# Four score matmuls of one burst: the two even key tiles first, then the two odd ones

## The chip, the cores and the metric

The kernel runs on one core of one Trainium2 chip. The metric is device time in microseconds (us) of one launch. Three runs of the kernel before gave 11260.99, 11263.95 and 11266.25 us, and the median, 11263.95 us, is the time before. Engines are named as in the profile: PE is TensorE's matmul and PEld its weight load, DVE is VectorE, ACT is ScalarE, POOL is GpSimd, SP is SyncE.

## The reference

Four graph layers follow one another on x (3327 rows, 128 columns) with one dense matrix adj (3327 by 3327). The change lies in layer 0, which takes almost all of the time. Cut to what matters (h is the normed x, and spatial_encoding and edge_encoding are both adj):

```python
q = (h @ Wq.T).reshape(d, n, heads_h)      # d = 128, n = 3327, heads_h = 8
k = (h @ Wk.T).reshape(d, n, heads_h)
v = (h @ Wv.T).reshape(d, n, heads_h)
a = jnp.einsum('dnh,dmh->dnm', q, k) * d ** -0.5
a = a + adj + adj
a = jax.nn.softmax(a, axis=2)
out = jnp.einsum('dnm,dmh->dnh', a, v).reshape(n, heads_h * d)
x = x + out @ Wo.T
```

So there are 128 heads, each with a contraction over only 8 elements, and for every head a 3327 by 3327 matrix of scores, of which every element goes through an exponential. Layers 1 to 3 are three more products with adj or its transpose and some elementwise work.

## The kernel before

**Tiles.** Scores are made transposed: keys lie on the 128 partitions, queries along the free dimension. There are 26 key tiles of 128 keys, taken as 13 pairs of an even and an odd tile (`NQ = 13`), 7 chunks of 476 queries (`NC`, `CW`; the last has 472), and 32 groups of 4 heads (`NG`). One unit of work, `u`, is (chunk, group, pair of key tiles): 7 x 32 x 13 = 2912 units. Each unit goes through its 4 heads j = 0 to 3 one after the other.

**One unit's banks.** A unit holds two of seven PSUM banks of the tile S, one for its even and one for its odd key tile (`banks(u)`). DVE first copies the adjacency of the tile into the bank (`seed`, L660). Then, for each head, PE adds the scores on top of what is in the bank (`scores`, L666), and ACT reads the bank and writes the exponential to SBUF (`exps`, L678 for both banks in one instruction of 128 x 952, L681 where the two banks don't lie side by side in the right order or one is left to DVE, 128 x 476). Heads 1 to 3 don't begin from the seed again: the queries' tile QS holds the negated query of the head before beside the new one, so the matmul takes the old head's score out of the bank and adds the new one. So a head's score matmul has to wait for the exponential of the head before on the same bank, and head 0's for the seed.

**Row halves.** A score matmul contracts over 64 rows only (two f32r halves of query and key, and old and new head). The even key tile's operands lie in partitions 0 to 63, the odd one's in partitions 64 to 127 (`KT[b][64 * r:64 * r + 64, ...]`, r = 0 even, r = 1 odd). The two therefore use the upper and the lower half of the array's rows.

**Values.** With the exponentials as moving operand, PE sums out the values and the softmax's denominator (`values`, L719): for one key tile four matmuls of 9 columns, one for each head, each at another 32-column group of the array, into one bank `po`. DVE empties `po` after the 13 units of a group (`store`, L727). In three of 13 units the odd tile's exponential of head 0 is worked out on DVE as a polynomial (`hand_exp`, L692 to L703).

**The order of the work.** It is written out by hand under a manual schedule: each engine runs its instructions in the order in which the loop issues them. The loop runs over slots i. ACT has one (unit, head) per slot: unit u has its heads in slots 4u, 4u + 3, 4u + 6 and 4u + 9 (`in_slot`). PE's work is issued in odd slots: a burst of four score matmuls, for the slots i + 1 and i + 2, then the values of one key tile of an earlier unit:

```python
if at % 2:
    for k in (1, 2):
        u, j = in_slot(i + k)
        if 0 <= u < n:
            scores(u, j)
    u, r = ((i - 11) // 4, 0) if at == 3 else ((i - 13) // 4, 1)
    if 0 <= u < n:
        values(u, r)
```

One call of `values` is one key tile of one unit, four matmuls; each f32 matmul of them leaves two records. So one burst and its values make one PE cycle: four records of L666, then eight of L719. There are two such cycles for each unit, 5824 in all.

Names for what follows: in a burst, A is the unit and head of slot i + 1 and B those of slot i + 2. Ae is A's even tile, Ao its odd one, Be and Bo are B's. Before, the burst runs Ae, Ao, Be, Bo. A and B are different units and never share a bank. In the bursts with i % 4 = 3, A is a unit's head 0, so that Ae and Ao wait for the two seeds; in all others A waits for the exponential of slot i - 2. B always waits for the exponential of slot i - 1. `touch` sets these dependencies bank by bank.

Of the kernel before, what the change touches and what calls it, by code (L numbers as in the profile page):

```python
# [22 lines left out]
P = 128  # L23
# [15 lines left out]
NG = HEADS // 4  # L39
# [41 lines left out]
def width_of(c):  # L81

    return min(CW, N + 1 - c * CW)
# [8 lines left out]
def gnn_kernel(ctx: ExitStack, tc: tile.TileContext, x, adj, Wq, Wk, Wv, Wo, embed, layer,  # L92
               embed_bias, layer_bias, weight, bias, W_in, W_out, out):
    nc = tc.nc
# [174 lines left out]
    class Square:  # L269
# [29 lines left out]
        def store(self, to=by_tile):  # L299
            nc.sync.dma_start(to[:, :, self.s * P:(self.s + 1) * P].rearrange("t p n -> p t n"), self.cols)  # L300
# [152 lines left out]
    with tc.tile_pool(name="d1", bufs=1) as d1, tc.tile_pool(name="d2", bufs=2) as d2, \  # L453
# [17 lines left out]
        with tc.If(loose > 0):  # L471
            for s in range(squares_of(0), NT):
                square(d2, s, d2)
            for t in range(NT):
# [5 lines left out]
                with tc.For_i(0, HEADS, 1) as d:  # L480
# [3 lines left out]
                    for r in range(2):  # L484
                        for b in range(4):
# [4 lines left out]
                                             start=True, stop=True)  # L490
# [9 lines left out]
            for c in range(NC):  # L500
                c0 = c * CW
                w = min(CW, N - c0)
# [3 lines left out]
                with tc.For_i(0, HEADS, 1) as d:  # L506
# [12 lines left out]
                    for t in range(NT):  # L519
# [8 lines left out]
                                         start=(t == 0), stop=(t == NT - 1))  # L528
# [9 lines left out]
    with tc.tile_pool(name="e1", bufs=1) as e1, tc.tile_pool(name="e_adj", bufs=30) as e_adj, \  # L538
# [5 lines left out]
        KT = [e1.tile([P, 3, NQ * P], F32R, name=f"KT{i}") for i in range(2)]  # L544
        QS = [e1.tile([P, 4, CW], F32R, name=f"QS{i}") for i in range(2)]
# [69 lines left out]
        with tc.If(loose < 1), tc.manual_schedule():  # L615
# [11 lines left out]
            n = len(pairs)  # L627
            adj_of, shift_of, v_of, e_of, here = {}, {}, {}, {}, {}
# [4 lines left out]
            def banks(u):  # L633
                odd = (4 - 2 * u) % 7
                return (odd + 1) % 7, odd
# [5 lines left out]
            after = mybir.DependencyInfo(mybir.DependencyClass.Sync, mybir.DependencyReason.DATA)  # L641

            def touch(u, rows, x):
                of = {banks(u)[r] for r in rows}
                for y, other in touched:
                    if not of & other and x.ins.engine != y.ins.engine:
                        tc.declare_no_dep(x.ins, y.ins, reason="other banks")
                for i in of:
                    if i in last:
                        tc.add_manual_dep(x.ins, last[i].ins.name, after, reason="the same bank")  # L650
                    last[i] = x
                touched.append((x, of))

            def bank(u, r):
                return S[:, banks(u)[r], :width_of(pairs[u][0])]

            def seed(u, r):
                c, g, q = pairs[u]
                w = width_of(c)
                touch(u, [r], nc.vector.tensor_copy(bank(u, r), adj_of[c][2 * q + r][:, :w]))  # L660

            def scores(u, j):
                c, g, q = pairs[u]
                w, b = width_of(c), (c * NG + g) % 2
                for r in range(2):
                    x = nc.tensor.matmul(  # L666
                        bank(u, r), KT[b][64 * r:64 * r + 64, max(0, j - 1), q * P:(q + 1) * P],
                        QS[b][64 * r:64 * r + 64, j, :w], start=False, stop=True, skip_group_check=True)
                    if (j, q, r) == (0, 0, 0):
                        tc.add_manual_dep(x.ins, here.pop(c * NG + g).ins.name, after, reason="the loads")  # L670
                    touch(u, [r], x)

            def exps(u, j):
                w, (even, odd) = width_of(pairs[u][0]), banks(u)
                e = e_of[u, j] = e_e.tile([P, 2, CW], F32, name=f"e{j}", bufs=(5, 4, 3, 2)[j])
                hand = j == 0 and by_hand(u)
                if even > odd and not hand:
                    touch(u, (0, 1), nc.scalar.activation(e[:, :, :w], S[:, odd:even + 1, :w], AF.Exp, scale=2.0))  # L678
                    return
                for r in range(1 if hand else 2):  # L680
                    touch(u, [r], nc.scalar.activation(e[:, 1 - r, :w], bank(u, r), AF.Exp, scale=2.0))  # L681

            def by_hand(u):

                return 0 <= u < n and pairs[u][2] in (0, 4, 8)

            def hand_exp(u):

                w = width_of(pairs[u][0])
                f, whole = (e_h.tile([P, CW], F32, name=f"h{i}")[:, :w] for i in range(2))  # L690
                power, e = whole.bitcast(I32), e_of[u, 0][:, 0, :w]
                touch(u, [1], nc.vector.tensor_scalar(f, bank(u, 1), LOG2_E2, EXP_LEAST, op0=ALU.mult, op1=ALU.max))  # L692
                yield
                nc.vector.tensor_scalar(whole, f, ROUNDER, ROUNDER, op0=ALU.add, op1=ALU.subtract)  # L694
                yield
                nc.vector.tensor_tensor(f, f, whole, op=ALU.subtract)  # L696
                yield
                nc.vector.tensor_scalar(power, whole, EXP_BITS, 2.0 ** 23, op0=ALU.add, op1=ALU.mult)  # L698
                for k in (4, 3, 2, 1):
                    yield  # L700
                    nc.vector.scalar_tensor_tensor(e, f if k == 4 else e, EXP_C[k], f, op0=ALU.add, op1=ALU.mult)  # L701
                yield
                nc.vector.scalar_tensor_tensor(e, e, EXP_C[0], power.bitcast(F32), op0=ALU.add, op1=ALU.mult)  # L703
# [11 lines left out]
            def values(u, r):  # L715
                c, g, q = pairs[u]
                w, k = width_of(c), c * NG + g
                for j, (v, of) in enumerate(heads_of(u, r)):
                    nc.tensor.matmul(po[32 * j:32 * j + H + 1, :w], VA[k % 2][:, 2 * pairs[v][2] + of, j, :],  # L719
                                     e_of[v, j][:, 1 - of, :w], start=(q == 0 and r == 0),  # L720
                                     stop=(q == NQ - 1 and r == 1))
# [11 lines left out]
            def loads(u):  # L733

                c, g, q = pairs[u]
                k = c * NG + g
                if k + 1 < NC * NG:
                    nxt = divmod(k + 1, NG)
                    if q == 1:
                        load_qk(*nxt)  # L740
                        v_of[k + 1] = load_v(*nxt)
                    if q == 4:
                        negate_q(*nxt)
                        spread_v(*nxt, v_of.pop(k + 1))
                        here[k + 1] = all_here(*nxt)
                if c + 1 < NC and (g, q) == (0, 0):
                    plan_squares(c)
                if g == NG - 1 and c + 1 < NC:
                    if q == 0:
                        shift_of[c + 1] = load_shift(c + 1)  # L750
                        adj_of[c + 1] = []
                    while len(adj_of[c + 1]) < min(NT, 2 * q + 6):
                        adj_of[c + 1].append(load_adj(c + 1, len(adj_of[c + 1]), shift_of[c + 1]))
# [30 lines left out]
            def in_slot(i):  # L784

                j = -i % 4
                return (i - 3 * j) // 4, j


            for i in range(-4, 4 * n + 15):  # L790
                u, j = in_slot(i)
                if 0 <= u < n:
                    exps(u, j)
                at = i % 4
                if i == -4:
                    seed(0, 0)
                if at == 0 and by_hand(i // 4):
                    by_vector.append(hand_exp(i // 4))
                if at == 0 and by_vector:
                    for k in range(2 if by_hand(i // 4) else 3):  # L800
                        if by_vector and next(by_vector[0], True):
                            by_vector.popleft()
                if at == 0 and i > 0:
                    for f, a in behind.pop(i // 4, ()):
                        f(*a)
                if at == 1 and (i + 3) // 4 < n:
                    seed((i + 3) // 4, 1)
                u = (i - 14) // 4
                if at == 2 and 0 <= u < n and pairs[u][2] == NQ - 1:
                    store(u)  # L810
                if at == 2 and (i + 6) // 4 < n:
                    seed((i + 6) // 4, 0)
                if at % 2:
                    for k in (1, 2):
                        u, j = in_slot(i + k)
                        if 0 <= u < n:
                            scores(u, j)
                    u, r = ((i - 11) // 4, 0) if at == 3 else ((i - 13) // 4, 1)
                    if 0 <= u < n:
                        values(u, r)  # L820
                if at == 0 and 0 <= i // 4 < n:
                    loads(i // 4)
# [110 lines left out]
    def arr(name, w=D):  # L933
        return big.tile([P, NT, w], F32, name=name)
# [175 lines left out]
    with tc.tile_pool(name="h1", bufs=1) as h1:  # L1110
# [23 lines left out]
        u, rr = arr("y"), sm.new()  # L1134
# [88 lines left out]
```

## Time and profile before

| what | before |
|---|---|
| median of three runs | 11263.95 us (11260.99 to 11266.25) |
| span of the profiled execution, first to last instruction | 11258.3 us |
| score matmuls (L666) | first at 451.7 us, last at 10294.8 us, 23296 of them |
| value matmul records (L719) | 46592 |
| ACT busy in the span | 10112.0 us (90%) |
| PE busy in the span | 10755.5 us (96%) |
| DVE busy in the span | 8348.1 us (74%) |
| mean granted TensorE clock | 0.976 |

The profile is of one execution with a span of 11258.3 us; the median of the runs is 5.65 us more, which holds what lies around the span and the scatter between runs. Busy is the union of an engine's records. A record begins when the instruction is taken up, so a record of ACT that is queued behind another is longer than the time it adds, and the ends of PE's records are modelled. Distances between the starts of neighbouring instructions say more than the lengths of records.

### The profile page before, as it was taken

What the parts mean: (1) busy time and instruction counts of PE and PEld (TensorE: products, weight loads), DVE (VectorE), ACT (ScalarE), POOL (GpSimd) and SP (SyncE); (2) the same over time, 40 slices, a digit from 0 to 9 for tenths busy, and PEclk for the clock granted to TensorE, in tenths of its full rate; (3) what the DMA queues carried; (4) which work ended last, traced back from release to release, by engine and by line L of the source; (5) the groups of instructions that cost most, each with busy time, mean ns of one, the idle gap of its engine ahead of it and who ended that gap; (6) DMA issues with size and microseconds to landing.
All of it is one profiled execution on the core that took longest, in us unless ns stands there. A gap on an engine that the chain in (4) does not pass through costs nothing.

```text
span 11258.3 us, 205583 instructions
## 1 busy us (share of the span) xinstructions
PE 10755.5 (96%) x72980; PEld 3651.8 (32%) x72980; DVE 8348.1 (74%) x13563; ACT 10112.0 (90%) x13718; POOL 2069.4 (18%) x3417
## 2 busy tenths in 40 slices
PE   4599999999999999999999999999999999998779
PEld 2133333333333333333333333333333333334444
DVE  5577877778777787777877778777777777777633
ACT  3599999999999999999999999999999999996210
POOL 5221211212112121111211222111221111111000
PEclk7799999999999999999999999999999999999889
DMA  8755555555555554555555555555554545444457
GB/s 247 247 101 97 96 97 115 100 98 96 97 116 99 100 97 82 111 97 101 99 92 116 96 102 99 92 116 96 102 92 84 108 80 85 81 84 121 158 183 272
DMA packets 732444, 1280.87 MB, mean 114 GB/s; under 512 B 190463, under 2 KB 607751, under 8 KB 714909
## 3 DMA queue, kind: packets, MB, share of 16 engines
q1 hardware_dynamic: 689528, 1138.10, 51.0%
q0 software_dynamic: 41888, 129.51, 3.9%
q8 instruction: 591, 9.68, 0.4%
q14 instruction: 437, 3.57, 0.1%
HBM read 1082.90 MB, written 184.09 MB: 113 GB/s over the span
## 4 chain that ended last, share of the span: by engine, by line
ACT 71%; issue 11%; PE 9%; DVE 3%; DMA 1%; POOL 0%; SPq 0%; DVEq 0%; POOLq 0%; ACTq 0%
ACT e L678 60%; ACT e L681 12%; PE pu L1016 5%; PE po L719 2%; PE S L666 1%; DVE e L701 1%; DVE S L660 1%; PE pu L968 0%; DMA ot<-oT_d 0%; DVE xs L1003 0%; PE pu L991 0%; DVE h L696 0%; PE pu L979 0%; DMA rows<-in_adj_dram 0%; DVE h L698 0%
## 5 line engine op out<-in xcount | busy, mean ns | idle before, releaser
L678 ACT ACTIVATE e<-S 128x952 f32<-128x952 f32 (+1 forms) x9408 | 8770.7, 1185 | 27.1 <-PE S L666 25.9
L719 PE MATMUL po<-e,VA 128*9 128x476 f32 (+1 forms) x46592 | 5739.4, 565 | 19.8 <-DVE OS L727 1.1
L660 DVE COPY S<-a 128x476 f32<-128x476 f32 (+1 forms) x5824 | 3816.2, 655 | 1960.3 <-ACT e L678 1486.5
L666 PE MATMUL S<-QS,KT 64*128 64x476 f32 (+1 forms) x23296 | 4846.9, 450 | 60.4 <-DVE S L660 50.6
L666 PEld LDWEIGHTS S<-QS,KT 64*128 64x128 f32 x23296 | 2426.4, 183 | 5175.9 <-issue 1638.6
L681 ACT ACTIVATE e<-S 128x476 f32<-128x476 f32 (+1 forms) x3808 | 2438.5, 795 | 7.7 <-PE S L666 7.2
L701 DVE SCALAR_TENSOR_TENSOR e<-e,h 128x476 f32<-128x476 f32 (+1 forms) x2016 | 1400.6, 695 | 46.1
L731 POOL DMA_DIRECT2D oT_d<-OS x896 | 471.7, 532 | 4589.4 <-DVE OS L727 4505.6
L719 PEld LDWEIGHTS po<-e,VA 128*9 128x9 f32 x46592 | 691.1, 88 | 1574.7 <-issue 1482.0
L576 POOL TENSOR_SCALAR QS<-QS 32x476 fp32r<-32x476 f32 (+1 forms) x1344 | 847.9, 631 | 1492.9 <-DMA QS<-qS_d 792.6
L692 DVE TENSOR_SCALAR h<-S 128x476 f32<-128x476 f32 (+1 forms) x672 | 439.2, 654 | 81.3 <-PE S L666 9.0
L701 DVE SCALAR_TENSOR_TENSOR e<-h 128x476 f32<-128x476 f32 (+1 forms) x672 | 452.6, 673 | 0.0
L696 DVE TENSOR_TENSOR h<-h,h 128x476 f32<-128x476 f32 (+1 forms) x672 | 443.7, 660 | 0.0
L703 DVE SCALAR_TENSOR_TENSOR e<-e,h 128x476 f32<-128x476 f32 (+1 forms) x672 | 437.3, 651 | 0.0
L134 ACT COPY uT<-pu 128x494 f32<-128x494 f32 (+1 forms) x12 | 6.5, 546 | 425.9 <-PE pu L1016 425.9
L586 POOL COPY VA<-VR 128x832 f32<-128x832 f32 x224 | 202.0, 902 | 984.8 <-DMA VR<-v_d 681.6
L1016 PE MATMUL pu<-strip,h 128*128 128x494 f32 (+2 forms) x728 | 294.0, 565 | 38.9 <-ACT h L949 38.9
L694 DVE TENSOR_SCALAR h<-h 128x476 f32<-128x476 f32 (+1 forms) x672 | 312.6, 465 | 23.2
L1016 PE MATMUL pu<-strip,y 128*128 128x494 f32 (+2 forms) x728 | 294.1, 566 | 28.9 <-DVE y L1003 17.8
L698 DVE TENSOR_SCALAR h<-h 128x476 int32<-128x476 f32 (+1 forms) x672 | 288.9, 430 | 23.0
L307 POOL TENSOR_TENSOR cols<-cols,on_all 128x256 f32<-128x256 f32 x286 | 258.4, 937 | 0.2
L293 DVE STREAM_TRANSPOSE cols<-rows 128x416 f32<-128x416 f32 x208 | 204.2, 986 | 21.4 <-DMA rows<-in_adj_dram 13.7
(186 smaller groups left out, 2449.3 us busy)
## 6 DMA issues: line engine op xcount, KB each, us to landing
KT<-kS_d SPq DMA_DIRECT2D x1792, 208.0 KB
KT<-kS_d SPq DMA_DIRECT2D x1792, 104.0 KB
VR<-v_d SPq DMA_DIRECT2D x224, 416.0 KB
strip<-adjT POOLq DMA_DIRECT2D x39, 1663.5 KB, 7.0
strip<-adjT SPq DMA_DIRECT2D x36, 1663.5 KB
QS<-qS_d SPq DMA_DIRECT2D x3072, 14.9 KB
QS<-qS_d SPq DMA_DIRECT2D x1536, 29.8 KB
adjT<-cols SPq DMA_DIRECT2D x26, 1664.0 KB
```

The source lines that it names most:

```text
L576: nc.gpsimd.tensor_scalar(QS[b][r0:r0 + 32, j + 1, :w], QS[b][r0:r0 + 32, j, :w].bitcast(F32), -1.0, 0.0, op0=ALU.mult, op1=ALU.add)
L660: touch(u, [r], nc.vector.tensor_copy(bank(u, r), adj_of[c][2 * q + r][:, :w]))
L666: x = nc.tensor.matmul(bank(u, r), KT[b][64 * r:64 * r + 64, max(0, j - 1), q * P:(q + 1) * P], QS[b][64 * r:64 * r + 64, j, :w], start=Fa ...
L678: touch(u, (0, 1), nc.scalar.activation(e[:, :, :w], S[:, odd:even + 1, :w], AF.Exp, scale=2.0))
L681: touch(u, [r], nc.scalar.activation(e[:, 1 - r, :w], bank(u, r), AF.Exp, scale=2.0))
L692: touch(u, [1], nc.vector.tensor_scalar(f, bank(u, 1), LOG2_E2, EXP_LEAST, op0=ALU.mult, op1=ALU.max))
L696: nc.vector.tensor_tensor(f, f, whole, op=ALU.subtract)
L701: nc.vector.scalar_tensor_tensor(e, f if k == 4 else e, EXP_C[k], f, op0=ALU.add, op1=ALU.mult)
L703: nc.vector.scalar_tensor_tensor(e, e, EXP_C[0], power.bitcast(F32), op0=ALU.add, op1=ALU.mult)
L719: nc.tensor.matmul(po[32 * j:32 * j + H + 1, :w], VA[k % 2][:, 2 * pairs[v][2] + of, j, :], e_of[v, j][:, 1 - of, :w], start=(q == 0 and r ...
L731: nc.gpsimd.dma_start(oT_d[:, d * N + c * CW:d * N + c * CW + w], o[32 * j:32 * j + H + 1, :w])
L1016: nc.tensor.matmul(pu[c][:, :w], y[:m, t, :], s[:m, c * AW:c * AW + w], start=(t == 0), stop=(t == NT - 1))
```

## The change

The four score matmuls of one burst are the same, on the same operands and banks. Their order changes from Ae, Ao, Be, Bo to Ae, Be, Ao, Bo. To that end the function `scores` loses its inner loop over the two tiles and takes the tile as an argument, and the burst's loop has the tile outside and the slot inside. Nothing else changes; the dependencies of each matmul are set by the same rule as before.

```diff
-            def scores(u, j):
+            def score(u, j, r):
                 c, g, q = pairs[u]
                 w, b = width_of(c), (c * NG + g) % 2
-                for r in range(2):
-                    x = nc.tensor.matmul(
-                        bank(u, r), KT[b][64 * r:64 * r + 64, max(0, j - 1), q * P:(q + 1) * P],
-                        QS[b][64 * r:64 * r + 64, j, :w], start=False, stop=True, skip_group_check=True)
-                    if (j, q, r) == (0, 0, 0):
-                        tc.add_manual_dep(x.ins, here.pop(c * NG + g).ins.name, after, reason="the loads")
-                    touch(u, [r], x)
+                x = nc.tensor.matmul(
+                    bank(u, r), KT[b][64 * r:64 * r + 64, max(0, j - 1), q * P:(q + 1) * P],
+                    QS[b][64 * r:64 * r + 64, j, :w], start=False, stop=True, skip_group_check=True)
+                if (j, q, r) == (0, 0, 0):
+                    tc.add_manual_dep(x.ins, here.pop(c * NG + g).ins.name, after, reason="the loads")
+                touch(u, [r], x)
...
                 if at % 2:
-                    for k in (1, 2):
-                        u, j = in_slot(i + k)
-                        if 0 <= u < n:
-                            scores(u, j)
+                    for r in range(2):
+                        for k in (1, 2):
+                            u, j = in_slot(i + k)
+                            if 0 <= u < n:
+                                score(u, j, r)
                     u, r = ((i - 11) // 4, 0) if at == 3 else ((i - 13) // 4, 1)
                     if 0 <= u < n:
                         values(u, r)
```

In the built program's order of instructions, SP's stands unchanged, and those of the other engines differ in line numbers, buffer numbers and, on PE, in the order within the bursts.

## The prediction

> **What bounds the kernel now.** I read the page first: shares of the engines, then the chain that ended last, then the groups.
>
> ```profile
> PE 10755.5 (96%) x72980; PEld 3651.8 (32%) x72980; DVE 8348.1 (74%) x13563; ACT 10112.0 (90%) x13718; POOL 2069.4 (18%) x3417
> ...
> ACT 71%; issue 11%; PE 9%; DVE 3%; DMA 1%; POOL 0%; SPq 0%; DVEq 0%; POOLq 0%; ACTq 0%
> ...
> L678 ACT ACTIVATE e<-S 128x952 f32<-128x952 f32 (+1 forms) x9408 | 8770.7, 1185 | 27.1 <-PE S L666 25.9
> L666 PE MATMUL S<-QS,KT 64*128 64x476 f32 (+1 forms) x23296 | 4846.9, 450 | 60.4 <-DVE S L660 50.6
> L681 ACT ACTIVATE e<-S 128x476 f32<-128x476 f32 (+1 forms) x3808 | 2438.5, 795 | 7.7 <-PE S L666 7.2
> ```
>
> The chain runs over ACT, and ACT's two exponential lines waited only 35 us for anything. But PE shows 96% too, so the question is which of the two is full. Busy shares don't tell; the busy time by windows says the same of the middle of the stage:
>
> ```profile
> 2000.00:4000.00 2000.00, 1990.79 (x14220) 635.35 (x14219) 1582.67 (x2545) 1996.61 (x2689) 394.58 (x651) 1.00 0.56 101
> ```
>
> (PE 1990.79, PEld 635.35, DVE 1582.67, ACT 1996.61, POOL 394.58 of 2000 us, granted clock 1.00.) What decides is the distance between starts, from the timeline in narrow windows. ACT first (start, length, instruction):
>
> ```profile
> 5009.63 1.19 ACT L678 ACTIVATE e<-S 128x952 f32<-128x952 f32 x1
> 5010.47 1.20 ACT L678 ACTIVATE e<-S 128x952 f32<-128x952 f32 x1
> ...
> 5012.16 0.83 ACT L681 ACTIVATE e<-S 128x476 f32<-128x476 f32 x1
> 5012.60 2.95 ACT L678 ACTIVATE e<-S 128x952 f32<-128x952 f32 x3
> ```
>
> A wide exponential is followed after 0.84 us though its record says 1.19, a narrow one after 0.44. Over all records between 1000 and 9800 us the medians of these distances are 0.844 and 0.447. ACT's own need for one PE cycle (two slots) is (9408 x 0.844 + 3808 x 0.447) / 5824 = 1.656 us. The stage has 10294.8 - 451.7 = 9843 us for 5824 cycles, 1.690 each (1.6885 between 1000 and 9800 us). So ACT is full to within 0.033 us a cycle.
>
> PE, an undisturbed cycle, by narrow windows of the timeline:
>
> ```profile
> 5009.79 0.48 PE L666 MATMUL S<-QS,KT 64*128 64x476 f32 x2
> 5010.11 0.38 PE L666 MATMUL S<-QS,KT 64*128 64x476 f32 x2
> 5010.41 0.57 PE L719 MATMUL po<-e,VA 128*9 128x476 f32 x1
> 5010.82 0.58 PE L719 MATMUL po<-e,VA 128*9 128x476 f32 x4
> 5011.33 0.48 PE L666 MATMUL S<-QS,KT 64*128 64x476 f32 x1
> ```
>
> Ae and Ao start together at 5009.79, Be and Bo together 0.32 us later, the first four value records 0.30 after that, the second four after 0.41, the next burst after 0.51: 1.54 us. So PE can go round in 1.54 and is made to go round in 1.69; its slack is 0.15 us a cycle. That is little, and the change spends PE time.
>
> **The change, part by part.** *The order.* Number, shapes and weights of the instructions stay; nothing is added on any engine, and no DMA moves. What changes is which neighbours can run together. Ae and Ao stand on different row halves and start in the same moment; four matmuls take two steps. In the new order Ae and Be are neighbours on the same half, so Be can't start before Ae has streamed; Ao, behind Be in PE's order, starts with Be; and Bo is on Ao's half and must wait for Ao's stream. That is three steps: Ae, then Be with Ao, then Bo. One step more.
>
> *What a step costs.* A burst at 5013.09 shows the loads of weights too (engine PEld, then PE):
>
> ```profile
> 5013.09 0.19 PEld L666 LDWEIGHTS S<-QS,KT 64*128 64x128 f32 x2 [0.80 <-ACT e L681]
> 5013.20 0.19 PEld L666 LDWEIGHTS S<-QS,KT 64*128 64x128 f32 x2
> ...
> 5013.09 0.48 PE L666 MATMUL S<-QS,KT 64*128 64x476 f32 x2
> 5013.41 0.37 PE L666 MATMUL S<-QS,KT 64*128 64x476 f32 x2
> ```
>
> The first pair's matmul records last 0.48 us, the second pair's 0.37: the first hold their weight load, 0.11 us, since they begin with it. The second pair's loads begin at 5013.20, when the first pair begins to stream, so they lie beside a stream on their own row half, and the matmuls follow at 5013.41. The stream alone is then 0.32 - 0.11 = 0.21 us. With three decimals from the records of 5211 bursts: first to third matmul 0.322 (lower quartile, where nothing else is waited for; the least is 0.314), load 0.107 (the two load rows above, 5013.091 and 5013.198), step 0.322 - 0.107 = 0.215 us. Bounds: 0.314 - 0.107 = 0.207 below; above, a step with its load exposed, 0.322.
>
> *A rule that speaks to it.* The row just shown has weights loaded beside a stream on the same half. The Trainium skill (TensorE: Matmul & The Clock Gate, Part 3, The mechanism) says the opposite for this case, that a weight load overlaps running matmuls only if its row group is another one (though it also speaks of a background weight buffer). By that rule the new step would cost 0.322 and the time would be the second rival's below. I go by the row.
>
> *The new PE cycle.* The fastest quarter of cycles lies at 1.548 or less, so 1.548 + 0.215 = 1.763 us, against ACT's need of 1.656 and today's 1.6885. PE becomes the bound. If ACT and DVE never delayed it: (1.763 - 1.6885) x 5824 = +434 us.
>
> *Waits that stay.* In 31% of the cycles today Ao starts over 0.1 us after Ae (0.25 on average; these are mostly bursts in which A is a head 0 and waits for the odd seed), and those cycles take 1.828 us on average. In them the new order costs nothing: Be fits into the gap before Ao. 22% of all cycles are already longer than 1.763. If each of these kept its length and all others went to 1.763, the mean would be 1.788; if ACT's queue evens them out over four cycles (two units), the mean of the larger of the two is 1.768. I take 1.768, since ACT then has 0.11 us a cycle in hand: +0.0795 x 5824 = +463 us. The outer value 1.788 gives +580.
>
> *The wait that is added to A.* Ao now stands behind Be, and Be waits for the exponential of slot i - 1, while A's exponential is the next but one on ACT. Queued behind Be are Ao, Bo and the eight value records. The loop: Be and Ao start, 0.37 us to the end of Ao's record, 0.04 to ACT's start (commonest distance in the records where ACT was waiting), 1.07 for a wide exponential that was not queued, 0.05 from its end to a weight load, 0.11 for the load: 1.64 us. That is under 1.763, so PE's cycle hides it, with 0.12 to spare. Were PE not the bound, it would still lie under today's 1.6885, by 0.05.
>
> *Seeds.* Two DVE copies of 0.655 us a unit keep their order. A longer cycle gives DVE more time (80% busy in the window above), so I cost this at zero; if a copy comes late, it delays a burst as today, which is in the 1.788.
>
> *The sum*, against the profiled execution: 11258.3 + 463 = 11721, and with the 5.65 us between the span and the median 11727 us. Outside the stage (before 451.7, after 10294.8 us) nothing changes.
>
> **The rivals.** *The step with its load exposed.* If Bo's weights can't be loaded before Ao has streamed, or Be's before Ae has, a step costs 0.322 and the cycle 1.548 + 0.322 = 1.870: +1057 us, some 12320 us. For it: no burst of today has two neighbours on the same half with nothing between, so the loads' place in such a sequence is inferred. Against it: the loads at 5013.20, which stand ahead of matmuls that can't start until 5013.41. Half of the bursts exposed would give 1.822, +777 us, 12041.
>
> *Not slower: the new order fills the gap before Ao.* Be runs while Ao waits for its seed. If the third step is worth less than the slack (0.14 us a cycle, 1.6885 - 1.548), PE stays below ACT, and what is left is less waiting of ACT; at best its 0.033 us a cycle is won, 192 us, 11072 us. The point is a step of 0.14 us; the row above has 0.21, and 69% of the cycles have no gap to fill. So this needs a stream to be shorter than the records show.
>
> *The change does nothing.* If the two halves' matmuls in truth ran one after the other and only their records start together, the order would be immaterial: 11264 us. Against it: the third matmul starts 0.32 us after both others, while one that is late by itself is followed 0.32 later by the next on its own half, so the halves have clocks of their own.
>
> **How the numbers follow.** Load hidden, PE bound: 70%, with times from 1.525 + 0.207 = 1.732 a cycle (the least cycle and the least step; +253 us, 11517) to 1.788 (11844), likeliest 11727. Load exposed in some or all bursts: 16%, half of it below 12041. Not slower: 8%, of which 5% faster by more than 0.2% and 3% within it. No effect: 2%. Something slower than 12041 not thought of: 4%. The range 11517 to 12041 holds 70% + 8%, about 8 in 10. A difference of 0.2% (23 us) is about what a measurement of this kernel can tell from none. Faster 5%, same 5%, slower 90%.
>
> **What would show it.** Right: in narrow windows of the timeline a burst begins with one matmul record of about 0.48, two start together 0.32 later, one 0.21 after these, and the values 0.30 after that; the least cycle is 1.75 to 1.76; ACT's exponentials get idle time before them released by PE's L666, about 0.1 us a cycle, 650 us in all; the chain goes over PE. Wrong: if the fourth matmul starts 0.32 after the third, the load is exposed; if all four start within two steps, PE doesn't keep the order I think; if ACT still has no idle time, the step is hidden.

## The result, and the profile after

The changed kernel takes 11448.15 us (median of 4 runs, 11446.09 to 11449.27) against 11263.42 us before on the same footing: 185 us more, a ratio of 1.0165 with a 95% interval of 1.0152 to 1.0177. The forecast was slower, and it was slower; but the forecast had 463 us, 2.5 times what came.

From the page of the changed kernel (L665 is now the score matmul, L677 and L680 the exponentials, L718 the values):

```profile
PE 10974.5 (96%) x72980; PEld 3867.6 (34%) x72980; DVE 8336.5 (73%) x13563; ACT 10177.7 (89%) x13718; POOL 2072.9 (18%) x3417
...
PE 89%; DVE 3%; ACT 3%; issue 1%; DMA 0%; POOL 0%; SPq 0%; DVEq 0%; POOLq 0%; ACTq 0%
...
L677 ACT ACTIVATE e<-S 128x952 f32<-128x952 f32 (+1 forms) x9408 | 8540.6, 1030 | 146.2 <-PE S L665 135.8
L665 PE MATMUL S<-QS,KT 64*128 64x476 f32 (+1 forms) x23296 | 5077.5, 429 | 38.5 <-DVE S L660 30.3
```

The chain went from ACT 71% to PE 89%, which looks like a full PE. The third row speaks against it: a full PE would have left ACT some 650 us of idle time, as the forecast put it, and its wide exponentials waited for 146, nearly all of it on the score matmul. Their records also got shorter, 1030 ns where they had 1185: fewer of them stand queued behind another.

How bursts look now, by narrow windows of the timeline, one burst from 4999.37 and one from 5002.48:

```profile
4999.37 0.49 PE L665 MATMUL S<-QS,KT 64*128 64x476 f32 x2
4999.70 0.39 PE L665 MATMUL S<-QS,KT 64*128 64x476 f32 x2
...
4999.37 0.19 PEld L665 LDWEIGHTS S<-QS,KT 64*128 64x128 f32 x2 [0.80 <-DVE S L660]
...
5001.36 0.66 DVE L660 COPY S<-a 128x476 f32<-128x476 f32 x1
5001.67 0.97 ACT L677 ACTIVATE e<-S 128x952 f32<-128x952 f32 x1
5002.48 0.48 PE L665 MATMUL S<-QS,KT 64*128 64x476 f32 x1
5002.69 0.18 PEld L665 LDWEIGHTS S<-QS,KT 64*128 64x128 f32 x2
5002.70 0.48 PE L665 MATMUL S<-QS,KT 64*128 64x476 f32 x2
5003.02 0.38 PE L665 MATMUL S<-QS,KT 64*128 64x476 f32 x1
```

In the first, two matmuls start together and two more 0.33 us later: two steps, as before the change. The first two start 7 ns apart, and the second of them is Ao: in this burst A is a head 0, and in the trace both of the first two weight loads wait for DVE's semaphore (number 100), that of the seeds, while the other two wait for ACT's (117). PE began Ao beside Ae, past Be, which stands ahead of it and is on Ae's half. In the second burst Ae starts alone; 0.21 us later two weight loads come at once, and a matmul with its load (0.48 us) with them. There Be's wait for the exponential of slot i - 1 wasn't met (that record ends at 5002.64, and the loads come 0.05 later), and Ao stood behind it, though its own seed had ended at 5002.02.

The second kind is the common one. Between 1000 and 9800 us Ao starts over 0.1 us after Ae in 72% of the bursts (0.23 on average), where it was 31% before. In the bursts with i % 4 = 1, where no seed is waited for, that is 1637 of 2557, and none of 2606 before; in these the next matmul starts 0.056 us (median) after the end of the exponential that Be waits for. In both kernels, in nearly all cycles, the next burst starts 0.92 us after the first value record. What varies is the time from a burst's start to its values: 0.772 us on average before and 0.805 after. So many bursts do take a third step, in whole or in part, and a cycle grows by only 0.033 us: before the change too, in 75% of the bursts, Be's exponential had not released it when the burst began, and PE waited there.

What that does to ACT shows where a unit's odd exponential is made on DVE, so that ACT has one narrow exponential by itself, then a wide one, then A's of the burst below. The same place before and after (start, length):

```profile
2541.12 0.83 ACT L681 ACTIVATE e<-S 128x476 f32<-128x476 f32 x1
2541.57 1.25 ACT L678 ACTIVATE e<-S 128x952 f32<-128x952 f32 x1
2542.07 0.48 PE L666 MATMUL S<-QS,KT 64*128 64x476 f32 x2
2542.38 0.37 PE L666 MATMUL S<-QS,KT 64*128 64x476 f32 x2
2542.59 1.08 ACT L678 ACTIVATE e<-S 128x952 f32<-128x952 f32 x1
```

```profile
2584.86 0.66 ACT L680 ACTIVATE e<-S 128x476 f32<-128x476 f32 x1
2585.31 1.06 ACT L677 ACTIVATE e<-S 128x952 f32<-128x952 f32 x1
2585.81 0.49 PE L665 MATMUL S<-QS,KT 64*128 64x476 f32 x2
2586.13 0.38 PE L665 MATMUL S<-QS,KT 64*128 64x476 f32 x2
2586.54 0.96 ACT L677 ACTIVATE e<-S 128x952 f32<-128x952 f32 x1 [0.17 <-PE S L665]
```

The first block is the kernel before. Ae and Ao end at 2542.55 (2542.07 + 0.48), and A's exponential starts 0.04 us later, at 2542.59, while Be and Bo still run. In the second, the kernel after, Ae and Ao end at 2586.29 and A's exponential starts at 2586.54: 0.04 after Be's end (2586.50 in the record), 0.25 after Ao's. ACT was idle for 0.17 us. A's exponential needs Ae and Ao alone, but PE's completions are counted in its own order, and Be now comes before Ao. Among all bursts with two steps, 430 had a wide exponential of A for which ACT sat idle over 0.02 us; none began sooner than 0.040 us after the end of the third matmul (median 0.045), nor sooner than 0.239 after the second's. So A's scores are known to ACT one step later, 0.21 us. The two blocks show a second delay too: the burst starts 0.12 us after the end of the lone narrow exponential before the change (2541.95 to 2542.07) and 0.29 after it (2585.52 to 2585.81).

The ends of ACT's records show how much of that counts. Between 1000 and 9800 us the median distance from one end to the next is 0.857 us for a wide exponential and 0.459 for a narrow one, in both kernels. What the ends are late by, over these medians, is 21 us in all before and 185 us after (8800 us of the stage). 153 of the 185 lie at one place: the second exponential after a narrow one by itself, 422 times of 422, 0.36 us on average. Before, it is late there once in 430.

### The profile page after: what moved, and what is told of

Its sections match the earlier page's. It is cut to its first block, busy times and chain, and to the rows that moved or that the text cites. A ratio compares the mean times of both kernels' runs of the same rounds, so it can differ in the third digit from the quotient of the medians.

```text
span 11447.0 us, 205551 instructions
## 1 busy us (share of the span) xinstructions
PE 10974.5 (96%) x72980; PEld 3867.6 (34%) x72980; DVE 8336.5 (73%) x13563; ACT 10177.7 (89%) x13718; POOL 2072.9 (18%) x3417
## 4 chain that ended last, share of the span: by engine, by line
PE 89%; DVE 3%; ACT 3%; issue 1%; DMA 0%; POOL 0%; SPq 0%; DVEq 0%; POOLq 0%; ACTq 0%
PE po L718 44%; PE S L665 38%; PE pu L1016 5%; ACT e L677 2%; DVE e L700 1%; DVE S L660 1%; ACT e L680 0%; PE pu L968 0%; PE ps_y L912 0%; DVE xs L1003 0%; DVE OS L726 0%; PE pu L991 0%; PE pu L979 0%; DMA ot<-oT_d 0%; DVE h L695 0%
## 5 line engine op out<-in xcount | busy, mean ns | idle before, releaser
L677 ACT ACTIVATE e<-S 128x952 f32<-128x952 f32 (+1 forms) x9408 | 8540.6, 1030 | 146.2 <-PE S L665 135.8
L718 PE MATMUL po<-e,VA 128*9 128x476 f32 (+1 forms) x46592 | 5738.5, 565 | 4.3
L665 PE MATMUL S<-QS,KT 64*128 64x476 f32 (+1 forms) x23296 | 5077.5, 429 | 38.5 <-DVE S L660 30.3
L665 PEld LDWEIGHTS S<-QS,KT 64*128 64x128 f32 x23296 | 2641.8, 184 | 4865.1 <-ACT e L677 1371.3
L680 ACT ACTIVATE e<-S 128x476 f32<-128x476 f32 (+1 forms) x3808 | 2156.8, 664 | 8.7 <-PE S L665 8.3
L718 PEld LDWEIGHTS po<-e,VA 128*9 128x9 f32 x46592 | 692.6, 88 | 1854.7 <-issue 1772.0
```

The lines of the kernel that those rows point to most:

```text
L665: x = nc.tensor.matmul(bank(u, r), KT[b][64 * r:64 * r + 64, max(0, j - 1), q * P:(q + 1) * P], QS[b][64 * r:64 * r + 64, j, :w], start=Fa ...
```

## The experiments

Differences are against the kernel before as timed beside each group of runs (11258.63, 11262.63 and 11259.14 us). The theories, in the order in which I held them. H (row halves): three steps, as forecast. W (waits): PE passes Be if nothing but the row half holds it, and the order matters only through waits. W2: these waits close a loop of two slots that limits the common cycle. W3: they make A late in every cycle, but ACT only runs dry where a lone narrow exponential lets it get ahead.

**PE alone as the bound, in both orders.** Half of the exponentials are left out, chosen so that B never has to wait for one. Two score matmuls then follow each other on a bank with no exponential between; the first lines leave out the dependency between them, as both are PE's.

```diff
                 for i in of:
-                    if i in last:
+                    if i in last and last[i].ins.engine != x.ins.engine:
                         tc.add_manual_dep(x.ins, last[i].ins.name, after, reason="the same bank")
...
             def exps(u, j):
+                if j % 2 == 0:
+                    return
                 w, (even, odd) = width_of(pairs[u][0]), banks(u)
-                e = e_of[u, j] = e_e.tile(...)
+                e = e_of[u, j] = e_of[u, j - 1] = e_e.tile(...)
...
             def by_hand(u):
-                return 0 <= u < n and pairs[u][2] in (0, 4, 8)
+                return False
```

Old order: 

> Old order (Ae, Ao, Be, Bo), but ACT makes the exponentials of heads 1 and 3 only; the values of heads 0 and 2 use those of 1 and 3, and no exponential is made on DVE. Left out: half of the exponentials. ACT's need for a cycle falls from 1.656 to under 0.9 us, and B (head 1 or head 3, after a head without an exponential) waits for no exponential any more, so PE is the bound. Both theories: a cycle near PE's least, 1.54 to 1.62 us, that is 1415 us outside the stage plus 5824 x 1.54 to 1.62 = 10385 to 10850 us.

New order: 

> The same with half of the exponentials left out, in the new order (Ae, Be, Ao, Bo). Theory W (the order matters only through waits: PE begins Ao beside Ae although Be stands between them, and is held up only where Be has to wait for an exponential): no wait stands before Ao, so the time is that of half_alt within 1%, and the records show two matmuls starting together, then two more 0.32 us later. Theory H (row halves, my forecast: Be behind Ae on the same half holds Ao back, three steps): 0.215 us more a cycle, 5824 x 0.215 = 1250 us, 12% over half_alt, and no two matmuls at the start of a burst start together.

Measured: 10466.7 us (10465.99 to 10467.01) and 10474.49 us (10472.26 to 10476.16), 0.07% apart, where theory H wanted 1250 us. A burst of the new order:

```profile
5001.35 0.19 PEld L665 LDWEIGHTS S<-QS,KT 64*128 64x128 f32 x2 [0.80 <-DVE S L660]
5001.46 0.19 PEld L665 LDWEIGHTS S<-QS,KT 64*128 64x128 f32 x2
...
5001.35 0.49 PE L665 MATMUL S<-QS,KT 64*128 64x476 f32 x2
5001.67 0.38 PE L665 MATMUL S<-QS,KT 64*128 64x476 f32 x2
```

Over 5471 cycles the second matmul starts 6.8 ns after the first on average (3.4 ns in the old order), the third 0.322 us after it in both, and the mean cycle is 1.555 against 1.552 us. The first two loads both wait for DVE's semaphore, so they are Ae's and Ao's. With PE as the bound and no wait in the way, the order costs 8 us. Theory H is out.

**The wait alone, with the halves alternating.** (In short:)

```diff
# order Ae, Ao, Be, Bo
+ Ao: tc.add_manual_dep(x.ins, last[banks(B)[0]].ins.name, after)   # what Be waits for
```

> Old order (Ae, Ao, Be, Bo) with one thing added: Ao also waits for the exponential that Be waits for (slot i - 1). The halves alternate as before. Theory W: slower than before, since A's exponential now hangs on the exponential of slot i - 1; less than the 185 us of the change, because Be's end is not in A's way: 30 to 120 us. Theory H: the halves alternate, there are two steps, so no change beyond 0.2% (23 us).

Measured: 11293.46 us, a ratio of 1.003 (1.0018 to 1.0041), 35 us. Ao's place behind the wait costs something with the halves as before, but a fifth of the change only.

**Ao last.**

```diff
-                    for r in range(2):
-                        for k in (1, 2):
+                    for k, r in ((1, 0), (2, 0), (2, 1), (1, 1)):
```

> Order Ae, Be, Bo, Ao. Ao now stands behind Bo on its own half and behind Be's wait. Theory W: the loop from one exponential over Be's wait to the end of Ao and on to A's exponential grows by one stream, some 0.2 us, from 1.71 to some 1.9 us a cycle at most; the evening out over cycles takes part of it: 400 to 1100 us more than before, several times the 185 us. Theory H counts steps: Ae, then Be with Bo, then Ao, three steps as in the change, so about the 185 us of the change again.

Measured: 11553.7 us, a ratio of 1.0261 (1.0245 to 1.0276), 295 us: over the 185 of theory H and under what I gave theory W. The loop that I reckoned with is 0.05 us from an exponential's end to Be's release, 0.70 to Ao's end, 0.04 to ACT and the exponential. I had taken the latter as 1.06 us; but part of that was waiting behind the exponential before. In this kernel the mean wide record is 0.969, which makes 1.76 us, and the median cycle is 1.754, half of all between 1.744 and 1.765. So here the loop agrees with the common cycle, and a queued record taken for a latency is part of why the size was wrong (1.06 would still give 1.85, not 1.9).

**The two waits in the old order.** (In short:)

```diff
# order Ae, Ao, Be, Bo
+ exponential of A: tc.add_manual_dep(x.ins, be_of[u, j].ins.name, after)   # the end of Be
```

By itself: 

> Old order (Ae, Ao, Be, Bo) with one thing added: ACT's exponential of A also waits for the end of Be of the same burst, as it does in the new order, where Be stands before Ao and PE's count tells of both. Theory W2 (a loop of two slots: the exponential of slot i - 1 releases Be, the end of Be releases A's exponential, which is the exponential of slot i' - 1 for the next burst): slower than before by 60 to 150 us, since here Be starts to stream at once. Rival (only Ao's place behind the wait counts): no change, within 23 us.

With Ao's wait: 

> Old order with both things added: Ao waits for the exponential that Be waits for, and A's exponential waits for the end of Be. Theory W2: these two are all that the new order does to the time, so the 185 us of the change, 150 to 220, with the row halves alternating. Rival (row halves cost part of the 185 us, the waits the 35 us measured): 35 us again, at most 70.

Measured: 11310.56 us, 48 us (ratio 1.0043, 1.0029 to 1.0056), under what was expected; and 11416.33 us, 154 us (1.0135, 1.0119 to 1.015), as expected. The two apart make 35 and 48, together 154. So two waits, with the row halves alternating as before, make 154 of the 185 us. The other 31 us are not settled. The copy isn't exact: the added wait for Be also holds narrow exponentials of the even tile, which in the new order need Ae alone (28 that ACT waited for began before Be's end there).

**One kind of burst at a time.** (In short; `EVEN_FIRST` stands for the new order, `ALTERNATE` for the old.)

```diff
+                    for k, r in (EVEN_FIRST if at == 1 else ALTERNATE):     # and at == 3
```

> New order (Ae, Be, Ao, Bo) only in the bursts with i % 4 = 1, in which A is head 2 and B head 1; old order in the others. Theory W2: the loop runs through every burst, and each kind of burst gives part of it: 40 to 110 us. Rival (a step more in bursts without a gap before Ao): these bursts have no seed to wait for, so nearly all of the 185 us, 150 to 190.

> New order only in the bursts with i % 4 = 3, in which A is a head 0 that waits for the seeds and B head 3; old order in the others. Theory W2: 40 to 110 us. Rival (a step more in bursts without a gap before Ao): Ao waits for its seed in most of these bursts anyway, so 0 to 30 us.

Measured: 11308.51 us (46 us, ratio 1.0042, 1.0028 to 1.0056) and 11366.14 us (104 us, 1.0092, 1.0076 to 1.0107). My forecast had the bursts with a late seed (i % 4 = 3) cost nothing, since Be would fill the gap before Ao; they cost more than twice the others.

The place with the lone narrow exponential shows how these sums come about. In the table, the second column is the mean time from the end of the lone narrow exponential to the start of the burst over the late one, between 1000 and 9800 us:

| kernel | burst starts after, us | A's exponential waits for Be's end | late at that place, us in all |
|---|---|---|---|
| before | 0.11 | no | 0 |
| Ao's wait alone | 0.28 | no | 34 |
| end of Be alone | 0.11 | yes | 36 |
| both | 0.28 | yes | 109 |
| new order at i % 4 = 1 only | 0.11 | yes | 40 |
| new order at i % 4 = 3 only | 0.38 | no | 67 |
| the change | 0.38 | yes | 153 |

The late exponential is A of a burst with i % 4 = 1. What makes this burst start later is the burst before it (i % 4 = 3), where Ao is held until Be is released and Bo has to follow Ao: a third step. From the end of the exponential that releases Be to that burst's values it is 0.52 us on average before, 0.69 with Ao's wait alone, and 0.78 in the change (medians 0.51, 0.67 and 0.68); the next burst begins 0.92 us after these. To this Be's end adds 0.21. Before, A's scores came some 0.12 us early (0.17 + 0.21 less the 0.26 by which A is late with both), so each delay alone is mostly hidden and the two together are not. That is why 35 and 48 make 154, and why the new order in the bursts with i % 4 = 3 costs more than in the others. The start of 0.38 instead of 0.28 is the part of the open 31 us that shows; why some of the bursts before are longer still in the change is not settled.

**No lone narrow exponential.** That W2 couldn't hold showed in the ends of ACT's records: two wide exponentials need 2 x 0.857 = 1.714 us, so a common cycle of 1.716 is ACT at its own rate and no loop. W3 was what the place of the lateness said. The test takes the place away: all exponentials on ACT.

```diff
             def by_hand(u):
-                return 0 <= u < n and pairs[u][2] in (0, 4, 8)
+                return False
```

Old order: 

> Old order, and the odd tile's exponential of head 0 is made by ACT in all units, none on DVE. ACT's need rises: 0.857 us for a wide exponential and 0.459 for a narrow one (medians between the ends of records) make 1.714 us a cycle in six of seven units and 1.836 in the seventh, 1.731 on average where it was 1.685; 0.046 x 5824 = 270 us more than before, about 11530 us.

New order: 

> New order, with no exponential on DVE. Theory W3 (the new order makes A's scores known to ACT 0.2 us later in every cycle, but ACT only runs dry where a lone narrow exponential lets it get ahead, that is once in each unit by hand): without these units nearly all of the change's cost is gone, 0 to 60 us over nohand_alt. Theory W2 as I had it (a loop of 1.71 us that is the limit of the common cycle): the loop has no room to hide, since ACT's need was and is 1.714 in the common cycle, so something like the 185 us stays, at least 100.

Measured: 11495.66 us (11493.5 to 11504.37) and 11535.31 us (11527.05 to 11539.77). ACT's larger need costs the old order 237 us, a little under the 270 reckoned. On top of that the new order costs 40 us, where it cost 185. Its ACT groups:

```profile
L677 ACT ACTIVATE e<-S 128x952 f32<-128x952 f32 (+1 forms) x9984 | 9011.0, 1070 | 12.3 <-PE S L665 11.3
L680 ACT ACTIVATE e<-S 128x476 f32<-128x476 f32 (+1 forms) x3328 | 1930.1, 707 | 0.4 <-PE S L665 0.3
```

12 us of waiting for scores instead of 146; by the ends of its records ACT is late by 31 us, where the old order without exponentials on DVE has 2. Ao still starts over 0.1 us after Ae in 80% of the bursts, but ACT isn't there to wait for it. That is what W3 forecast. This pair alone doesn't single out the narrow exponential: it also gives ACT more work in the mean cycle, behind which PE's delays can hide, and takes the polynomial off DVE. The place of the lateness is what points at it.

## Why the forecast was wrong

- *What bounds the kernel now*: ACT, as said, but fuller than I had it. I took ACT's need from the distances between starts (0.844 and 0.447, 1.656 us a cycle). From the ends it is (8418 x 0.857 + 3407 x 0.459) / 5211 = 1.685, against a cycle of 1.6885: ACT had almost nothing to give.
- *The third step*: this is the step that failed. "Be can't start before Ae has streamed" holds; "Ao, behind Be in PE's order, starts with Be" doesn't, unless Be's wait is unmet. The row half by itself adds no step: 10474.49 against 10466.7 us, 8 us where 0.215 a cycle would have made 1250. Where Be's wait is unmet, in most bursts of the changed kernel, Ao does start with Be, but PE stood waiting there before as well: the mean burst grew by 0.033 us, not by 0.215 or the 0.0795 that was summed, and PE did not become the bound of the mean cycle. The common cycle is 1.716 us, ACT's own 1.714, and not 1.763. My own row had shown weight loads passing a matmul that couldn't start yet (5013.20); whether a matmul can pass one too I didn't ask.
- *The rule weighed against the row*: a load beside a stream on its own half is again what the runs show, since in the burst of PE alone the third matmul's load comes 0.11 us after the first's, while the first streams, and the matmul starts 0.322 us after the first with a record of 0.38, without its load. That agrees with the row, and not with the rule. (By the rule the time would have been that of the first rival; the prediction calls it the second.)
- *The wait that is added to A*: named, and priced at nothing because a PE cycle of 1.763 would hide it, and otherwise because its loop of 1.64 us lies under the mean cycle. PE's cycle did not become 1.763, and the delay does its harm at an uneven place that a mean cycle doesn't show; what was priced at nothing is nearly all there is, 154 of 185 us by the two waits alone. It was also put at Ao's end (0.37 us after its start) where it is Be's end, one step later in a burst of two steps.
- *Waits that stay* and the gap before Ao: wrong. The new order in just the bursts where it was to cost nothing costs 104 us.
- *Seeds*: DVE's own order is as it was, and no experiment took them alone.
- *The rivals*: neither the exposed load nor "not slower" came. "The change does nothing" is right for the row halves, and that is what one sees with ACT relieved; it is wrong for the waits.

## What to carry to other kernels

An order of instructions on one engine is first an order of waits and of completions: see what stands behind each unmet wait that didn't before, and what its consumer must now count past. A later result costs nothing while the consumer is queued, and what exceeds the slack where the consumer's work is short; two delays that share one slack cost more together than the sum of each alone. So look for the uneven place, not for the mean cycle. Where an engine's records are longer than the time they add, read its rate from their ends.

## What the runs showed of the hardware

- PE begins a matmul on one row half while an earlier one in its order still waits for the other half: 6.8 ns after the first of the burst, where a neighbour with none in between starts after 3.4 ns. It does not pass one whose semaphore isn't there: in the burst at 5002.48 Ao was taken up with Be, 0.21 us after Ae, and so were 1637 of 2557 in the bursts without a seed, 0.056 us (median) after the exponential that Be waits for.
- A wide exponential takes 0.96 us by itself and adds 0.857 when queued, while the mean record is 0.97 us (Ao last) to 1.33 (old order, none on DVE), by how full the queue is. In the kernel before, the starts of queued ones are mostly 0.844 apart where the ends are 0.857.
- ACT's start, when it waits for scores, comes 0.045 us (median) after the end of the last matmul that PE's count takes in, also one whose bank it doesn't read: 430 times, never sooner than 0.040.
